# Block products 1 and 5 of the first MLP's first layer at two levels, with later index constants and whole kept weight tiles

## The chip, the cores and the metric

The kernel runs on one core of a Trainium2 chip. The metric is the device time of one execution in microseconds, lower is better. The core has five engines with queues of their own: TensorE (PE; its weight loads are PEld), VectorE (DVE), ScalarE (ACT), GpSimd (POOL) and SyncE (SP). SyncE, ScalarE and GpSimd also issue DMAs. All arithmetic here is in float32.

## The reference

Four sequences of 512 tokens with 512 features go through an attention block with two MLPs, and then through an adapter chosen per sequence.

```python
q, k, v = x @ Wq, x @ Wk, x @ Wv
attn = softmax(einsum('btd,bTd->btT', q, k) * 512 ** -0.5)
attn_out = einsum('btT,bTd->btd', attn, v) @ Wp + bp
cms_out = gelu(attn_out @ cW1 + cb1) @ cW2 + cb2 + one_hot(target_codes)[:, None, :]
modifier = gelu(concatenate([attn_out, cms_out], -1) @ mW1 + mb1) @ mW2 + mb2
x = clip(x + cms_out + modifier, 0.0, 1.0)

# adapter of sequence b, with its expert e = stream[b]
h = gelu(x @ W_down[e] + b_down[e]) @ W_up[e] + b_up[e] + x
out = (h - mean(h)) * rsqrt(var(h) + 1e-5) * ln_w[e] + ln_b[e]
```

The shapes: Wq, Wk, Wv, Wp 512x512; cW1 512x2048; cW2 2048x512; mW1 1024x2048; mW2 2048x512; W_down 3x512x256; W_up 3x256x512. The gelu is the exact one.

## The kernel before

**Pairs and block products.** The four sequences are worked on in two pairs. The two sequences of a pair stand side by side as the two column halves of one right-hand matrix, with features on the partitions. So each large product is a 2x2 block product, and it is computed in seven block products in place of eight. They are numbered 1 to 7: 1, 2, 3 and 4 take a block of the weights as it is or a sum of all four, 5, 6 and 7 take sums or differences. The right side has four differences t1 to t4 (`token_sums`, L185): t1 = b12 - b11, t2 = b22 - t1, t3 = b22 - b12, t4 = b21 - t2. The weights have four sums s1 to s4 (`weight_sums`, L178). Product 5 is s1 with t1, 6 is s2 with t2, 7 is s3 with t3, 3 is s4 with b22, 4 is a22 with t4, and 1 and 2 are a11 with b11 and a12 with b21. Products 1, 2 and 4 are called PLAIN because their weights are blocks of the original.

**Two levels.** In cW2, mW1 and mW2 each of these seven products is again split into seven (`inner`, L556). An inner product is 128 columns of weights against 256 columns of tokens. `inner` copies its first product from PSUM with ScalarE into `first`, and seven additions by VectorE (L573, or L575 with a bias) put the rest together. Their order is fixed: 1, 5, 6, 7, 2, 3, 4. The layer of cW1 (`c1_layer`, L638) has one level only: per product two groups g of four tiles, each tile two matmuls of width 512 (L663). There products 1 and 5 are copied out by ScalarE (L669, L671), and the others are added by VectorE (`combine_first_tile`, L677).

**Weight sums ahead of time.** GpSimd computes all sums of cW1, cW2, mW1 and mW2 while attention runs, and stores them in DRAM (`c1_kept`, `c2_kept`, `m1_kept`, `m2_kept`). `expansion` (L311) holds cW1 (`expand_c1`, L200), cW2 and mW1. `late_expansion` (L320) holds mW2 and runs beside the first pair's mW1 layer. In `expand` (L267) a product that is not PLAIN is stored by three DMAs: two for its own columns, one for its sums. `inner_weights` (L326) loads a tile by SyncE into one of four `wslot` buffers of 1792 floats per partition, seven blocks each; a group of mW1 uses two such tiles.

**The front.** Wq and Wk are transposed and multiplied into one matrix, `w_qk`. Then x is transposed (`transposed`, L356; `evacuate` L102 copies from PSUM, in turn by VectorE and ScalarE), and `pair_product` (L453, matmuls at L469) multiplies w_qk by the pair. Its outer loop is over the two row halves r of each block, its inner one over the products 1, 2, 5, 6, 7, 3, 4. Then come scores and softmax (L496 to L519), and a second pair product. Small constants stand ahead of the first transposes of x in the program: positions, expert indices and one-hot targets (L406 to L430, L437 to L440), each a few elements wide and done by VectorE. Sequences 2 and 3 of x are loaded at the start by ScalarE's and SyncE's queues (L140).

**Order.** The program is recorded through a tile framework that sets semaphores and orders each engine's queue. `tc.keep_in_program_order` pins an instruction where it stands. Buffers rotate: eight PSUM banks (`bank`) and four `wslot`.

**The MLPs.** Per pair: cW1 layer, cW2 layer (`second_layer`, L786, matmuls L812), mW1 layer (`m1_layer`, L713, matmuls L728), mW2 layer (`second_layer` again). Between the last two, x^T is loaded from DRAM and added to `cms` by GpSimd (L1012 to L1017); `m_last` (L861) reads the sum from product 5 of the mW2 layer on, which is the third of its seven. The adapters of the first pair run in steps between the groups of the second pair's cW1 layer. The last pair's adapters stand at the end (`adapter`, L904): transposes, down, up, and per tile of 128 tokens the normalisation, with multiplication by ln_w on VectorE (L961), addition of ln_b on GpSimd (L962), and the store by SyncE (L963). The fourth tile has a shorter form on VectorE alone (L949, L953).

Of the kernel before, what the change touches and what calls it, by code (L numbers as in the profile page):

```python
# [18 lines left out]
def kernel(  # L19
# [51 lines left out]

    FIRST = (1, 5, 6, 7, 2, 3, 4)
# [23 lines left out]
    wslot = [const.tile([P, 1792], F32, name=f"wslot{i}") for i in range(4)]  # L96
# [43 lines left out]
    for b in range(2, B):  # L140
        x_rows.append(load_x(b, (nc.scalar, nc.sync)[b % 2], x_places[b]))

# [53 lines left out]


    c1_kept = [spill.tile([P, 4, 2, 256], F32, name=f"c1_kept{j}") for j in range(4)]

    def expand_c1(j):  # L200
        raw = slot[4 + j % 2].rearrange("p (c h n) -> p c h n", c=4, h=2)
        for h in range(2):
            nc.gpsimd.dma_start(
                out=raw[:, :, h, :],
                in_=cW1[:, h * HH + j * 256 : h * HH + (j + 1) * 256].rearrange(
                    "(c p) n -> p c n", p=P
                ),
            )
        s = (part.rearrange("p c n -> p (c n)"), slot[1])[j % 2].rearrange(
            "p (k c n) -> p k c n", k=4, c=2  # L210
        )
        weight_sums(
            raw[:, 0:2, 0, :], raw[:, 2:4, 0, :], raw[:, 0:2, 1, :], raw[:, 2:4, 1, :],
            s[:, 0], s[:, 1], s[:, 2], s[:, 3],
        )
        nc.gpsimd.dma_start(out=c1_kept[j], in_=s)
# [4 lines left out]
    KEPT = {1: 0, 2: 1, 4: 2, 5: 3, 6: 4, 7: 5, 3: 6}  # L221
    PLAIN = {1: (0, 0), 2: (1, 0), 4: (1, 1)}

    def kept(name, units):
        return {
            (p, u): spill.tile([P, 4 if p in PLAIN else 7, 2, P], F32, name=f"{name}_{p}_{u}")
            for p in range(1, 8)
            for u in range(units)
        }
# [4 lines left out]
    turn = [0]  # L234

    def four(t):
        return t.rearrange("p (k c n) -> p k c n", k=4, c=2)
# [4 lines left out]
    def block_sums(t):  # L242

        return t.rearrange("p (c n) -> p c n", c=4)

    def split(t):
        return [t[:, :1024], t[:, 1024:2048]]

    flat_mod, flat_part = ([t.rearrange("p c n -> p (c n)") for t in ts] for ts in (mod, [part]))
    spare = [split(flat_part[0]), [first.rearrange("p c n -> p (c n)")]]  # L250
    spare = [sums_of(t) for ts in spare for t in ts]

# [14 lines left out]
    def expand(unit, raw, outer, places, then):  # L267

        src, is_first, dst, u = unit
        raw = [t.rearrange("p (c n) -> p c n", c=4) for t in raw]  # L270
        s1, s2, s3, s4 = (block_sums(t) for t in outer)
        a11, a12, a21, a22 = (
            raw[0][:, :, :256], raw[1][:, :, :256], raw[0][:, :, 256:], raw[1][:, :, 256:]
        )
        nc.gpsimd.tensor_tensor(s1, a21, a22, ALU.add)
        nc.gpsimd.tensor_tensor(s2, s1, a11, ALU.subtract)
        nc.gpsimd.tensor_tensor(s3, a11, a21, ALU.subtract)
        nc.gpsimd.tensor_tensor(s4, a12, s2, ALU.subtract)
        blocks = {1: a11, 2: a12, 4: a22, 5: s1, 6: s2, 7: s3, 3: s4}
        for i, (p, a) in enumerate(blocks.items()):  # L280
            if i == len(PLAIN):

                then()
            to = places[i % len(places)]
            weight_sums(
                a[:, 0:2, :P], a[:, 2:4, :P], a[:, 0:2, P:], a[:, 2:4, P:],
                to[:, 0], to[:, 1], to[:, 2], to[:, 3],
            )
            d = dst[p, u]
            if p in PLAIN:  # L290
                nc.gpsimd.dma_start(out=d, in_=to)
            else:
                nc.gpsimd.dma_start(out=d[:, 0:2].rearrange("p k c n -> p (k c) n"), in_=a[:, :, :P])
                nc.gpsimd.dma_start(out=d[:, 2], in_=a[:, 2:4, P:])
                nc.gpsimd.dma_start(out=d[:, 3:7], in_=to)
            yield

    def expand_all(units, raw, outer, places):
        load_raw(*units[0][:2], units[0][3], raw)
        for n, unit in enumerate(units):  # L300

            def then():
                if n + 1 < len(units):
                    load_raw(*units[n + 1][:2], units[n + 1][3], raw)

            yield from expand(unit, raw, outer, places, then)
# [4 lines left out]
    def expansion():  # L311

        for j in range(4):
            expand_c1(j)
            yield
        c2_units = [(cW2, False, c2_kept, u) for u in range(2)]
        outer = split(slot[1]) + split(slot[3])
        yield from expand_all(c2_units + m1_units, slot[4:6], outer, spare)

    def late_expansion():  # L320

        outer = split(flat_mod[0]) + split(flat_mod[1])
        places = [sums_of(t) for t in split(slot[0])]
        yield from expand_all(m2_units, slot[6:8], outer, places)

    def inner_weights(src, is_first, store, p, u):  # L326

        w = next_weights().rearrange("p (k c n) -> p k c n", k=7, c=2)
        if p not in PLAIN:
            nc.sync.dma_start(out=w, in_=store[p, u])  # L330
            return w
        h, o = PLAIN[p]
        plain = w[:, 0:2].rearrange("p k c n -> p (k c) n")
        if is_first:
            at = o * HH + u * 256
            rows = src[h * V : (h + 1) * V, :].rearrange("(c p) n -> p c n", p=P)
            nc.sync.dma_start(out=plain, in_=rows[:, :, at : at + P])
            nc.sync.dma_start(out=w[:, 2], in_=rows[:, 2:4, at + P : at + 2 * P])
        else:
            at = o * 256  # L340
            rows = src[h * HH : (h + 1) * HH, :].rearrange("(c p) n -> p c n", p=P)
            for i in range(2):
                k = 4 * i + 2 * u
                nc.sync.dma_start(out=w[:, i], in_=rows[:, k : k + 2, at : at + P])
            nc.sync.dma_start(out=w[:, 2], in_=rows[:, k : k + 2, at + P : at + 2 * P])
        nc.sync.dma_start(out=w[:, 3:7], in_=store[p, u])
        return w
# [57 lines left out]

    pos = const.tile([P, NV], F32, name="pos")  # L406
    tc.keep_in_program_order(nc.vector.tensor_copy(pos, pos_i))

    code = const.tile([P, B], F32, name="code")
    tc.keep_in_program_order(nc.vector.tensor_copy(code, code_i))  # L410

    ex = const.tile([P, B], F32, name="ex")
    tc.keep_in_program_order(nc.vector.tensor_copy(ex, str_i))
    wrap = const.tile([P, B], F32, name="wrap")
    nc.vector.tensor_scalar(wrap, ex, 0.0, float(E), ALU.is_lt, ALU.mult)
    nc.vector.tensor_add(ex, ex, wrap)
    nc.vector.tensor_scalar(ex, ex, 0.0, float(E - 1), ALU.max, ALU.min)
    ex_v = const.tile([P, B], F32, name="ex_v")  # L420
    nc.vector.tensor_scalar(ex_v, ex, float(V), None, ALU.mult)
    ex_bn = const.tile([P, B], F32, name="ex_bn")
    nc.vector.tensor_scalar(ex_bn, ex, float(BN), None, ALU.mult)
    idx_e = const.tile([P, B], I32, name="idx_e")
    nc.vector.tensor_copy(idx_e, ex)
    idx_d = const.tile([P, B, NV], I32, name="idx_d")
    idx_u = const.tile([P, B, NB], I32, name="idx_u")
    for b in range(B):
        nc.vector.tensor_scalar(idx_d[:, b, :], pos, ex_v[:, b : b + 1], None, ALU.add)
        nc.vector.tensor_scalar(idx_u[:, b, :], pos[:, :NB], ex_bn[:, b : b + 1], None, ALU.add)  # L430

# [4 lines left out]

    target = const.tile([P, B, NV], F32, name="target")  # L437
    for b in range(B):
        nc.vector.tensor_scalar(target[:, b, :], pos, code[:, b : b + 1], None, ALU.is_equal)
        nc.vector.tensor_add(target[:, b, :], target[:, b, :], cb2_c)  # L440
# [12 lines left out]
    def pair_product(lhs, rhs, out, bias_c=None):  # L453

        for r in range(2):
            c11, c12, c21, c22 = (out[k][:, o + r, :] for o in (0, 2) for k in range(2))

            def total(dst, one, two, o):
                if bias_c is None:
                    add(dst, one, two)  # L460
                else:
                    nc.vector.scalar_tensor_tensor(
                        dst, one, bias_c[:, o + r : o + r + 1], two, ALU.add, ALU.add
                    )

            for p in (1, 2, 5, 6, 7, 3, 4):
# [11 lines left out]
                elif p == 2:  # L478
                    ps2 = ps
                elif p == 5:  # L480
                    nc.scalar.copy(c22, ps)
                elif p == 6:
                    add(c21, ps, c11)
                    total(c11, ps2, c11, 0)
# [38 lines left out]
    for pair in range(B // 2):  # L523
# [4 lines left out]
        for k in range(2):  # L528
            if s0 + k:
                transposed(chunks(x_rows[s0 + k]), xT[k])  # L530
            nc.scalar.dma_start(out=xT_kept[s0 + k], in_=xT[k])
        pair_product(lhs_qk, block_operands(*xT, mod), u)
        if pair == 0:
# [3 lines left out]
            lhs_vp = block_weights(w_vp, slot[2], nc.vector)  # L537
        steps(expanding, 6)
# [575 lines left out]
```

## Time and profile before

| what | us |
|---|---|
| median of 3 runs | 1232.78 (1230.43 to 1233.13) |
| profiled execution, its own time | 1232.73 |
| its span, first to last instruction | 1230.6 |

| stretch, us from the start | length | PE busy | DVE busy | POOL busy |
|---|---|---|---|---|
| 0 to 64.3: weights Q/K, x of pair 0, first pair product | 64.3 | 52.0 | 37.5 | 38.2 |
| 64.3 to 164.5: rest of attention, pair 0 | 100.2 | 98.7 | 48.7 | 95.1 |
| 164.5 to 284.5: attention, pair 1 | 120.0 | 114.3 | 69.0 | 119.6 |
| 284.5 to 380.6: cW1 layer, pair 0 | 96.1 | 96.1 | 60.8 | 53.7 |
| 380.6 to 465.2: cW2 layer | 84.6 | 84.6 | 79.4 | 3.4 |
| 465.2 to 634.4: mW1 layer | 169.2 | 169.2 | 129.9 | 96.8 |
| 634.4 to 720.7: mW2 layer | 86.3 | 85.4 | 84.0 | 23.2 |
| 720.7 to 848.1: cW1 layer of pair 1, with pair 0's adapters | 127.4 | 127.4 | 70.8 | 27.2 |
| 848.1 to 1102.1: cW2 and mW1 layers, pair 1 | 254.0 | 254.0 | 197.6 | 11.9 |
| 1102.1 to 1212.5: mW2 layer and start of the last adapters | 110.4 | 109.5 | 95.2 | 42.7 |
| 1212.5 to 1230.6: end of the last adapter | 18.1 | 7.1 | 10.8 | 7.8 |

The rows come from one query of busy time by stretches; the first and the last but one rows and pair 1's middle are sums of two. A busy TensorE is not TensorE at its peak: ends of matmuls are modelled, and its clock can be lowered. What costs time is a stretch in which TensorE's busy time is shorter than the stretch, and a stretch at a low clock.

### The profile page before, as it was taken

The page shows a single profiled execution, that of the slowest core. Times are in us where ns is not written, and L with a number is a line of the kernel's source. Part 1 is how long each engine was busy: PE and PEld are TensorE (multiplying, and loading weights), DVE is VectorE, ACT ScalarE, POOL GpSimd, SP SyncE. Part 2 cuts the span into 40 slices and gives each one's busy share as a digit, 9 for nine tenths or more (in the row PEclk, how much of TensorE's full clock was granted, in tenths as well). Part 3 has the DMA queues.
Part 4 walks back from the last instruction along what each step waited for, and adds up shares of the span by engine and source line. Part 5 has one row for each costly group of instructions (what it writes and reads, how often), then busy time and mean ns, then how long its engine had stood idle before and what let it go on. Part 6 is the DMA issues. An engine that isn't in the chain of part 4 may idle for free.

```text
span 1230.6 us, 12329 instructions
## 1 busy us (share of the span) xinstructions
PE 1198.2 (97%) x4497; PEld 838.7 (68%) x4497; DVE 883.7 (72%) x1101; ACT 211.9 (17%) x361; POOL 519.5 (42%) x542
## 2 busy tenths in 40 slices
PE   7899999999999999999999999999999999999996
PEld 5344444444447888888888864446888888888872
DVE  4763474464759896699699943769986578699957
ACT  1112111112141000002220023352000002220014
POOL 6689999999900006686310263100000000117124
PEclk9899999999999999999999999999999999999998
DMA  9943466549634657867645462223653444465601
GB/s 327 341 185 138 158 235 222 184 158 324 222 106 142 235 158 237 307 235 250 236 154 223 162 188 77 69 99 102 251 162 130 155 187 161 149 214 180 220 1 69
DMA packets 93212, 226.30 MB, mean 184 GB/s; under 512 B 8884, under 2 KB 45792, under 8 KB 90080
## 3 DMA queue, kind: packets, MB, share of 16 engines
q1 hardware_dynamic: 67264, 132.14, 31.7%
q0 software_dynamic: 22560, 80.79, 18.6%
q10 hardware_dynamic: 3328, 12.58, 2.6%
q8 instruction: 36, 0.59, 0.2%
q14 instruction: 24, 0.20, 0.0%
HBM read 166.75 MB, written 58.72 MB: 183 GB/s over the span
## 4 chain that ended last, share of the span: by engine, by line
PE 88%; DVE 10%; issue 1%; ACT 0%; DMA 0%; POOLq 0%; POOL 0%; DVEq 0%; ACTq 0%
PE i L728 28%; PE i L812 22%; PE c L663 16%; PE pair L469 7%; PE prod_ps L372 7%; PE scores L501 3%; DVE slot L192 2%; PE down_ps L920 2%; PE up_ps L932 2%; DVE hidden L748 2%; PE tr_ps L361 1%; DVE mod L192 1%; DVE mod L517 1%; DVE mod L573 1%; PE res_ps L911 1%
## 5 line engine op out<-in xcount | busy, mean ns | idle before, releaser
L728 PE MATMUL i<-slot,wslot 128*128 128x256 f32 x1184 | 260.8, 379 | 0.0
L728 PEld LDWEIGHTS i<-slot,wslot 128*128 128x128 f32 x1184 | 225.0, 190 | 30.6
L812 PE MATMUL i<-slot,wslot 128*128 128x256 f32 x896 | 204.1, 380 | 1.9 <-DVE mod L573 1.6
L812 PEld LDWEIGHTS i<-slot,wslot 128*128 128x128 f32 x896 | 169.7, 190 | 27.1 <-DVE mod L573 3.2
L812 PE MATMUL i<-hidden,wslot 128*128 128x256 f32 x576 | 132.1, 379 | 0.0
L663 PE MATMUL c<-slot,wslot 128*128 128x512 f32 x288 | 125.1, 592 | 0.0
L580 ACT COPY first<-i 128x256 f32<-128x256 f32 (+1 forms) x56 | 26.8, 479 | 551.0 <-PE i L812 284.0
L812 PEld LDWEIGHTS i<-hidden,wslot 128*128 128x128 f32 x576 | 109.4, 190 | 16.2 <-issue 1.4
L573 DVE TENSOR_TENSOR part<-i,part 128x512 f32<-128x512 f32 (+1 forms) x156 | 91.0, 591 | 39.5 <-PE i L728 27.2
L602 ACT ACTIVATE hidden<-hidden,bias 128x512 f32<-128x512 f32 x128 | 85.8, 715 | 100.7 <-DVE hidden L443 100.7
L1013 POOL DMA_DIRECT2D slot<-xT_kept x4 | 2.2, 558 | 236.5 <-PE i L728 214.4
L663 PEld LDWEIGHTS c<-slot,wslot 128*128 128x128 f32 x288 | 54.6, 190 | 68.4 <-issue 65.8
L443 DVE TENSOR_TENSOR hidden<-c,hidden 128x512 f32<-128x512 f32 x80 | 54.0, 685 | 55.4 <-PE c L663 55.3
L663 PE MATMUL c<-wide,wslot 128*128 128x512 f32 x160 | 69.3, 592 | 0.0
L265 POOL DMA_DIRECT2D slot<-in_L_cond_mW x24 | 18.1, 762 | 120.6 <-DVE slot L192 118.6
L1015 POOL TENSOR_TENSOR cms<-cms,slot 128x1024 f32<-128x1024 f32 x8 | 23.5, 2948 | 96.4 <-PE i L728 81.0
L192 DVE TENSOR_TENSOR slot<-hidden,slot 128x1024 f32<-128x1024 f32 x48 | 62.7, 1306 | 0.3
L192 DVE TENSOR_TENSOR slot<-hidden 128x1024 f32<-128x1024 f32 x48 | 62.7, 1306 | 0.0
L663 PEld LDWEIGHTS c<-wide,wslot 128*128 128x128 f32 x160 | 30.4, 190 | 37.8 <-issue 36.8
L501 PE MATMUL scores<-hidden,hidden 128*128 128x512 f32 x128 | 55.3, 592 | 0.0
L573 DVE TENSOR_TENSOR part<-i,first 128x512 f32<-128x512 f32 (+1 forms) x62 | 36.3, 589 | 26.1 <-PE i L728 16.6
L443 DVE TENSOR_TENSOR hidden<-hidden,hidden 128x512 f32<-128x512 f32 (+1 forms) x40 | 49.8, 1248 | 1.8
(241 smaller groups left out, 1799.3 us busy)
## 6 DMA issues: line engine op xcount, KB each, us to landing
wslot<-m_kept SPq DMA_DIRECT2D x48, 896.0 KB
wslot<-m_kept SPq DMA_DIRECT2D x36, 512.0 KB
wslot<-c_kept SPq DMA_DIRECT2D x16, 896.0 KB
slot<-in_L_cond_mW POOLq DMA_DIRECT2D x24, 512.0 KB
m_kept<-part POOLq DMA_DIRECT2D x20, 512.0 KB
slot<-in_L_cond_cW POOLq DMA_DIRECT2D x16, 512.0 KB
wslot<-c_kept SPq DMA_DIRECT2D x32, 256.0 KB
wslot<-in_L_cond_mW SPq DMA_DIRECT2D x60, 128.0 KB
```

The lines of the kernel that those rows point to most:

```text
L192: i = eng.tensor_tensor(out_, one, two, ALU.subtract)
L372: nc.tensor.matmul(ps, lhsT=lhs(c)[:, d * P : (d + 1) * P], rhs=rhs(c), start=(c == 0), stop=(c == 3),)
L443: nc.vector.tensor_tensor(dst, a, b, ALU.add)
L469: nc.tensor.matmul(ps, lhsT=lhs[p][:, c, r * P : (r + 1) * P], rhs=rhs[p][:, c, :], start=(c == 0), stop=(c == 1),)
L501: nc.tensor.matmul(ps, lhsT=u[:, c, t * P : (t + 1) * P], rhs=xT[:, c, :], start=(c == 0), stop=(c == NV - 1),)
L573: nc.vector.tensor_tensor(dst, ps, other, ALU.add)
L580: nc.scalar.copy(c1, p1)
L602: nc.scalar.activation(block[:, t, :], block[:, t, :], AF.Gelu, bias=bias_c[:, 8 * half + t : 8 * half + t + 1],)
L663: nc.tensor.matmul(ps, lhsT=lhs(c, t), rhs=rhs[p][:, c, :], start=(c == 0), stop=(c == 1),)
L728: nc.tensor.matmul(out_ps[:, j, :], lhsT=a[j][:, KEPT[q], c, :], rhs=now[q][:, c, :], start=(c == 0), stop=(c == 1),)
L748: i = nc.vector.tensor_tensor(out_[:, tiles, :], one[:, tiles, :], two[:, tiles, :], ALU.subtract)
L812: nc.tensor.matmul(ps[:, :256], lhsT=a[k // 2][:, KEPT[q], k % 2, :], rhs=now[q][:, k, :], start=(k == 0), stop=(k == 3),)
```

## The change

It does seven things.

1. In the cW1 layer products 1 and 5 are split a second time: each of two groups takes seven inner products of 128 columns of weights and 256 tokens on a contraction of 128, two tiles each. `inner` puts them together, with `mod[0]` for the copy. Product 2 comes first now and is copied out by ScalarE; product 1 is put together in `h[2]` and added to `h[0]`. Two more sets of four small differences (`inner_sums`) are made by VectorE. `wslot` grows to 2048 floats, and `expand_c1` makes the inner sums for products 1 and 5.
2. `pair_product` runs over the products outside and over the row halves inside. Both transposes of a pair are made before the stores of x^T.
3. The small constants are made after the first pair product, in `constants()`.
4. Sequences 2 and 3 of x are loaded by GpSimd, behind the first loads of cW1.
5. A kept tile holds the whole block of 1024 floats and its sums of 1024, so that one DMA stores it and one loads it; `expand` makes the products in another order.
6. x^T is added to `cms` by an accumulating DMA instead of a load and two additions.
7. In the last adapter GpSimd takes both the multiplication and the addition of tiles 0 and 1, and VectorE both of tile 2.

```diff
+    FIRST_C = (2, 1, 5, 6, 7, 3, 4)
-    wslot = [const.tile([P, 1792], F32, name=f"wslot{i}") for i in range(4)]
+    wslot = [const.tile([P, 2048], F32, name=f"wslot{i}") for i in range(4)]
-    for b in range(2, B):
-        x_rows.append(load_x(b, (nc.scalar, nc.sync)[b % 2], x_places[b]))
...
+    def expand_c1(u, then):
...
+        weight_sums(
+            raw[0][:, 0, 0, :], raw[0][:, 1, 0, :], raw[1][:, 0, 0, :], raw[1][:, 1, 0, :], *inner_sums
+        )
+        nc.gpsimd.dma_start(out=c1_inner[1, u], in_=slot[1][:, 1024:])
...
+        weight_sums(s1[:, 0, 0, :], s1[:, 0, 1, :], s1[:, 1, 0, :], s1[:, 1, 1, :], *inner_sums)
+        nc.gpsimd.dma_start(out=c1_inner[5, u], in_=slot[1])
...
-            (p, u): spill.tile([P, 4 if p in PLAIN else 7, 2, P], F32, name=f"{name}_{p}_{u}")
+            (p, u): spill.tile([P, 1024 if p in PLAIN else 2048], F32, name=f"{name}_{p}_{u}")
...
-            if p in PLAIN:
-                nc.gpsimd.dma_start(out=d, in_=to)
-            else:
-                nc.gpsimd.dma_start(out=d[:, 0:2].rearrange("p k c n -> p (k c) n"), in_=a[:, :, :P])
-                nc.gpsimd.dma_start(out=d[:, 2], in_=a[:, 2:4, P:])
-                nc.gpsimd.dma_start(out=d[:, 3:7], in_=to)
...
+        def plain(*blocks):
+            for p, a, t in blocks:
+                inner_sums(a, t[:, 1024:])
+                keep(p, t[:, 1024:])
+                yield
...
+        def full(*sums):
+            for p, t in sums:
+                inner_sums(block(t[:, :1024]), t[:, 1024:])
+                keep(p, t)
+                yield
...
+        load_c1(0)
+
+        for b in range(2, B):
+            x_rows.append(load_x(b, nc.gpsimd, x_places[b]))
...
+    def constants():
+
+        tc.keep_in_program_order(nc.vector.tensor_copy(pos, pos_i))
...
     def pair_product(lhs, rhs, out, bias_c=None):
-        for r in range(2):
-            c11, c12, c21, c22 = (out[k][:, o + r, :] for o in (0, 2) for k in range(2))
...
-            for p in (1, 2, 5, 6, 7, 3, 4):
+        for p in (1, 2, 5, 6, 7, 3, 4):
+            for r in range(2):
+                c11, c12, c21, c22 = (out[k][:, o + r, :] for o in (0, 2) for k in range(2))
...
             lhs_vp = block_weights(w_vp, slot[2], nc.vector)
+            constants()
...
+        one = {1: inner_sums(0, b11)}
+        minus(t1, b12, b11)
+
+        def rest():
+            one[5] = inner_sums(1, t1)
+            minus(t2, b22, t1)
+            yield
+            minus(t3, b22, b12)
+            minus(t4, b21, t2)
+            yield
...
-        for p in FIRST:
+        two_level, one_level, rest = rhs
+        for p in FIRST_C:
             for g in range(2):
                 w = next_weights()
-                if p in (1, 2, 4):
-                    k, o = {1: (0, 0), 2: (1, 0), 4: (1, 1)}[p]
+                if p in (1, 5):
...
+                    def matmuls(q, ps):
+                        out_ps = ps.rearrange("p (j n) -> p j n", j=2)
+                        for j in range(2):
+                            nc.tensor.matmul(
+                                out_ps[:, j, :],
+                                lhsT=a[:, place[q], j * P : (j + 1) * P],
+                                rhs=two_level[p][q][:, 0, :],
+                                start=True,
+                                stop=True,
+                            )
+                        return out_ps
...
+                    inner(
+                        matmuls,
+                        [[v[:, o, pair_of, t, :] for t in range(2)] for o in range(2)],
+                        256, tmp=mod[0],
+                    )
+                    if p == 1:
+                        for tiles in (pair_of, slice(4 + 2 * g, 6 + 2 * g)):
+                            add(h[0][:, tiles, :], h[0][:, tiles, :], h[2][:, tiles, :])
+                            gelu(h[0], 0, cb1_c, range(tiles.start, tiles.stop))
+                    yield
+                    continue
...
-            nc.vector.tensor_mul(h, h, aff[:, 1, :])
-            nc.gpsimd.tensor_tensor(h, h, aff[:, 2, :], ALU.add)
+
+            scale = nc.gpsimd if final and t < 2 else nc.vector
+            shift_by = nc.vector if final and t == 2 else nc.gpsimd
+            scale.tensor_tensor(h, h, aff[:, 1, :], ALU.mult)
+            shift_by.tensor_tensor(h, h, aff[:, 2, :], ALU.add)
...
         for s in range(2):
-            nc.gpsimd.dma_start(out=in_rows[2 + s], in_=xT_kept[2 * pair + s])
-            for d in (slice(0, 2), slice(2, 4)):
-                nc.gpsimd.tensor_tensor(
-                    cms[s][:, d, :], cms[s][:, d, :], in_rows[2 + s][:, d, :], ALU.add
-                )
+            nc.gpsimd.dma_start(out=cms[s], in_=xT_kept[2 * pair + s], accum_op=ALU.add)
```

## The prediction

> **What bounds the kernel now.** I read the page first, then TensorE's waits, then the chain of waits in order of time, then busy time by short stretches and the timeline where the waits lie.
>
> ```profile
> PE 1198.2 (97%) x4497; PEld 838.7 (68%) x4497; DVE 883.7 (72%) x1101; ACT 211.9 (17%) x361; POOL 519.5 (42%) x542
> ...
> PEclk9899999999999999999999999999999999999998
> ...
> PE 88%; DVE 10%; issue 1%; ACT 0%; DMA 0%; POOLq 0%; POOL 0%; DVEq 0%; ACTq 0%
> ```
>
> TensorE is the bound: 97% busy, 88% of the chain. So time goes only where matmuls go, where a gap of TensorE closes, or where its clock rises. Who makes it wait:
>
> ```profile
> PE pair L469 <- DVE hidden L106: 5.1, 1, 5.1
> PE pair L469 <- DVE mod L192: 5.1, 3, 2.3
> ...
> PE i L812 <- DVE mod L573: 1.6, 4, 0.4
> ```
>
> Columns: total us, times, longest. 10.2 us lie in the Q/K pair products (L469). From 280 us to 1213 us all waits add up to 1.8 us, none of them on a DMA. Around the first Q/K product, by stretches (length; PE, PEld, DVE, ACT, POOL busy; clock, DMA share, GB/s):
>
> ```profile
> 29.30:34.30 5.00, 0.00 (x0) 0.00 (x0) 4.95 (x19) 0.00 (x0) 2.44 (x3) 0.98 1.03 406
> 34.30:36.00 1.70, 1.69 (x2) 0.84 (x3) 1.67 (x4) 0.67 (x2) 1.14 (x1) 0.50 1.07 394
> ...
> 41.30:43.60 2.30, 0.00 (x0) 0.00 (x0) 2.27 (x3) 0.59 (x1) 2.28 (x3) 1.00 1.03 427
> 43.60:46.00 2.40, 2.40 (x4) 1.16 (x5) 2.15 (x1) 0.00 (x0) 2.34 (x3) 0.65 0.98 406
> ```
>
> Each gap is paid twice: TensorE stands, then runs at 0.50 to 0.65 of its clock. In the first gap VectorE works through the small constants, some of them very slowly, and x's evacuation waits behind them:
>
> ```profile
> 26.35 4.13 DVE L418 TENSOR_TENSOR ex<-ex,wrap 128x4 f32<-128x4 f32 x1
> ...
> 34.31 5.26 PE L469 MATMUL pair<-hidden,cms 128*128 128x512 f32 x8 [5.09 <-DVE hidden L106]
> ```
>
> Rates come from the chain, where these stages run without a gap (each written matmul makes two records):
>
> ```profile
> 140.59 24.03 PE pair L469 x56
> ...
> 284.62 96.13 PE c L663 x224
> ...
> 465.36 169.21 PE i L728 x784
> ```
>
> So a record of width 512 costs 96.13/224 = 0.429 us, one of width 256 costs 169.21/784 = 0.216 us, and an undisturbed pair product 24.03 us. The end is a chain over VectorE, GpSimd and SyncE:
>
> ```profile
> 1224.96 0.68 DVE L961 TENSOR_TENSOR hidden<-hidden,wide 128x512 f32<-128x512 f32 x1
> 1225.73 1.26 POOL L962 TENSOR_TENSOR hidden<-hidden,wide 128x512 f32<-128x512 f32 x1 [2.09 <-DVE hidden L961]
> 1227.02 0.33 SPq L963 DMA_DIRECT2D out<-hidden  x1
> ```
>
> **What the Trainium skill says.** "TensorE: Matmul & The Clock Gate", section "What's actually happening": the array's clock is halved after about 3.4 us of idleness and comes back after about as much work. The trace agrees in kind (0.50 after a 5.0 us gap), but already a 2.3 us gap brings 0.65; the measurement decides. "SBUF — State Buffer", section "Who interferes with whom": a VectorE instruction with two SBUF inputs, or in a two-port mode, contends with GpSimd for a port pair, and the loser blocks for the whole instruction; one PSUM and one SBUF input do not contend. The trace agrees: the four-element add above took 4.13 us while GpSimd added back to back. "DMA: Bandwidth & Descriptors", section "SWDGE vs HWDGE vs iDMA": a DMA that accumulates can only be issued by GpSimd. No run here shows one yet.
>
> **The change part by part.** The sum is made against the profiled execution's own 1232.73 us (span 1230.6), which is within 0.1 us of the median of 1232.78.
>
> *Two levels for products 1 and 5.* One product of cW1 takes 2 groups x 4 tiles x 2 = 16 matmuls of width 512, 32 records: 13.73 us. At two levels it is 2 x 7 x 2 = 28 of width 256, 56 records: 12.09 us; the built order of instructions shows these 28. 1.65 us less, for two products and two pairs: **-6.6 us**. For it VectorE gets seven additions per group (about 0.62 us in a row, as L443's 0.68 and L573's 0.59 show) where ScalarE copied, and for product 1 two additions of 128x1024 (1.25): 6.9 us per group of product 1, 4.3 of product 5, against 6.04 on TensorE. TensorE can run ahead by eight PSUM banks; walking the built order with these durations, a bank comes free 1 us or more before it is wanted in pair 0 (half of that if GpSimd stretches the additions), and in pair 1, where the adapters' steps lie between, the tightest are within 0.5 us. I charge **+0.5**. The operands cost eight more subtractions of 128x256 (some 0.4 each), under the 13.7 us of product 2, which now comes first and needs none.
>
> *Constants later, and both row halves of one product in a row.* Before, from the end of the transposes at 29.2 to the end of the product at 64.3: 35.1 us, where 24.03 suffice; 11.1 are lost. After, no constant stands before the evacuation, and the first difference is wanted after two products of two halves, 6.86 us, not 3.43. What is late next: two block sums stand before x's copies and GpSimd is busy at that time; at 1.6 us each (L182 took 1.8) TensorE starts about 1.5 us late, and the second difference may be 1 us late: -11.1 + 2.5 = **-8.6**. Pair 1: 167.96 to 196.91 is 28.95 against 24.03; less 0.5 for a late difference, **-4.4**. The constants move beside the first scores: some 11 us of VectorE as stretched before, 4 if not, at tile 0 of eight. VectorE's step per tile was 2.35 us (86.92 to 89.27) against 3.43 of TensorE, so it catches up some 1 us per tile. Between 0 and 7 us, taken **+1.5**. The like wait in pair 1 (VectorE's 5.03 us at 212.84, then a 2.5 us gap and 1.6 us of low clock) depends on where GpSimd's 2.36 us additions fall: between -4 and +4, taken **0**.
>
> *Whole kept tiles, x's later rows by GpSimd.* GpSimd issues seven DMAs fewer per expanded unit, and its work ends earlier; it is hidden (first kept tile of cW2 wanted at 380). The weights of an unfolded product are 1 MB, not 896 KB; two per 12.09 us. Hidden as SyncE's queue always waited for TensorE and not the reverse: **0**, to +30 if a load is late. x2 and x3 are wanted at 164; moved past the first loads of cW1 they land far earlier: 0.
>
> *Accumulating DMA for x.* It replaces a 1 MB load and GpSimd's two additions (2.95 us each), which stand on VectorE's port in the second MLP's second layer: there TensorE lost 1.8 us in five waits, and a little rate. It has from the last reader (about 600) to 670 in pair 0, and some 35 us in pair 1; the plain load took 8 us (633.15 to 641.15). Its speed is not shown: at double that it is still hidden; late by 30 us it would cost as much. **-1.8** (0 to -2.9).
>
> *Tail.* Tiles 0 and 1 lose a VectorE multiplication each (1.2 us), tile 2 ends with VectorE's 0.68 in place of GpSimd's 1.26 plus a handover, while GpSimd takes four operations, ending by about 1224. **-1.2** (0 to -2).
>
> Sum: -6.6 + 0.5 - 8.6 - 4.4 + 1.5 - 1.8 - 1.2 = -20.6, so 1232.7 - 20.6 = **1212**.
>
> **Rivals.**
> 1. VectorE becomes the bound where it is loaded. Constants beside the scores stop it for their 11 us (7 after catching up, 1.6 of clock), and the first layer's groups of product 1 run at VectorE's pace with stretched additions. For it: 72% busy, ops at three times their length. Against: both places have slack of tiles or banks. -20.6 + 9 gives 1221.
> 2. The front gains nothing, as GpSimd's sums of cW1 now stretch VectorE where it was free: only -6.6, -1.8, -1.2 and little else: 1224. For it: GpSimd works through from 18.8. Against: the removed work exceeds what stretching can add.
> 3. Slower: loads of the weights. Place: the 56 steps of cW2, mW1, mW2 (28 per pair) which take two 1 MB tiles per 12.09 us from four buffers, 173 GB/s where 152 were wanted. It decides from 20.6/56 = 0.37 us per step; at 0.6 it gives 1232.7 - 20.6 + 34 = 1246. For it: DMAs are 0.73 busy in the first half of mW1's layer in pair 0 (465 to 547 us). Against: no wait on a DMA after 5 us, and longer rows per packet.
> 4. The change not doing what it says: excluded for the matmuls by the built order.
>
> **How the numbers follow.** Forecast 0.66 (own range 1205 to 1218); rivals 1 and 2 together 0.20; rival 3 with a late accumulate 0.09; a chance near nothing lost or won, 0.05. The range of 8 in 10 leaves out rival 3 and takes most of 1 and 2: 1203 to 1222. 0.2% is 2.5 us, about what a measurement can tell here. Faster 0.88, the same 0.03, slower 0.09.
>
> **What would show it.** Right: the first layer's stretch without adapters about 93 us where 96.1 were; two Q/K products of 24 to 27 us with a clock near 1; no wait on a DMA in the MLPs; no GpSimd additions to cms; the last out DMA some 1 us sooner after the last matmul. Wrong: TensorE waiting on VectorE in the new inner products, on a weight tile, or before the transposes of the softmax.

## The result: slower, 1246.85 us, with the profile after

The changed kernel takes 1246.85 us (median of 6 runs, 1236.63 to 1254.08) against 1232.7 (1229.03 to 1236.08): ratio 1.0101, 95% interval 1.0069 to 1.0133. A second measurement gave 1241.38 and 1.0105 (1.0045 to 1.0165). The forecast was 1212. Times here are medians of all runs, while the ratios leave out runs more than 1.5% above a kernel's fastest (none of these twelve), so a ratio is not the quotient of two medians. The spread is news too: 18 us between runs, where the kernel before has 7. The profiled execution is the shortest, 1236.63 us with a span of 1234.8, so it shows only 3.9 of the 14 us lost.

From the page of the changed kernel (busy time of the engines, TensorE's clock, the chain that ended last):

```profile
PE 1193.0 (97%) x4593; PEld 858.1 (69%) x4593; DVE 932.8 (76%) x1164; ACT 209.3 (17%) x355; POOL 474.2 (38%) x501
...
PEclk9998979999999999999999999999999999999998
...
PE 80%; DVE 12%; issue 3%; DMA 3%; ACT 1%; POOL 1%; ACTq 0%; DVEq 0%; POOLq 0%
```

TensorE's work fell by 5.2 us (1198.2 to 1193.0) and the span still grew; its share of the chain went from 88 to 80%. So it waits more. TensorE's waits (total us, times, longest):

```profile
PE prod_ps L425 <- DVE hidden L107: 13.9, 6, 9.3
...
PE tr_ps L414 <- DVE hidden L499: 3.8, 2, 2.3
PE tr_ps L414 <- DVE hidden L520: 3.6, 4, 3.1
PE i L852 <- DMA wslot<-in_L_cond_mW: 1.5, 1, 1.5
PE i L746 <- DVE hidden L632: 0.9, 3, 0.4
```

The 10.2 us before the Q/K products have shrunk to 1.4. In their place stand 9.3 us after the first softmax and 7.4 at the end of the first pair's V product, both on VectorE. By stages, from the start of TensorE's groups in the timelines (us; the last two columns are the two kernels with GpSimd's sums cut, experiment 3):

| stage | before | after | before, no sums | after, no sums |
|---|---|---|---|---|
| start to first scores | 80.5 | 70.8 | 69.8 | 69.6 |
| first scores to first V product | 59.9 | 71.4 | 60.0 | 59.9 |
| V product to pair 1's scores | 56.5 | 64.3 | 51.6 | 51.6 |
| those scores to the first c layer | 87.5 | 86.2 | 84.0 | 84.0 |
| first c layer | 96.1 | 95.1 | 96.1 | 92.8 |
| to pair 1's c layer | 340.2 | 340.5 | 340.1 | 338.7 |
| pair 1's MLPs and the end | 509.8 | 506.5 | 509.9 | 506.0 |

The c layer is that of cW1. The two gains forecast for the front arrived (9.7 us in pair 0; the second Q/K product takes 24.8 us instead of 28.95). Next to them 11.5 us are lost in the first softmax and 12.0 between the V product and the second Q/K product. Here is the first loss, as VectorE and GpSimd show it in the timeline (start, duration, instruction):

```profile
87.52 0.16 DVE L573 RECIPROCAL inv<-total 128x1 f32<-128x1 f32 x1 [0.84 <-ACT mod L571]
87.72 8.26 DVE L574 TENSOR_SCALAR mod<-mod,inv 128x512 f32<-128x512 f32 x1
95.90 0.67 DVE L566 TENSOR_REDUCE top<-scores 128x1 f32<-128x512 f32 x1
```

```profile
85.89 0.57 POOL L301 DMA_DIRECT2D c_kept<-part  x1 [0.30 <-POOL part L181]
86.48 2.35 POOL L298 TENSOR_TENSOR slot<-part,slot 128x1024 f32<-128x1024 f32 x1
88.80 2.34 POOL L298 TENSOR_TENSOR wide<-slot 128x1024 f32<-128x1024 f32 x1
91.10 0.71 POOL L178 TENSOR_TENSOR wide<-slot 128x256 f32<-128x256 f32 x1
...
94.51 0.71 POOL L179 TENSOR_TENSOR slot<-slot,slot 128x256 f32<-128x256 f32 x1
95.18 0.57 POOL L301 DMA_DIRECT2D c_kept<-wide  x1
95.77 0.78 POOL L180 TENSOR_TENSOR slot<-slot 128x256 f32<-128x256 f32 x1
```

The softmax's multiplication, which takes 0.49 us where nothing holds it, takes 8.26: from inside a run of eight additions of GpSimd's until GpSimd leaves the run to issue a DMA. It ends 0.2 us after that issue, so its last 0.49 us begin inside it. The reduction behind it, which reads PSUM, is untouched. The first loss is made of this meeting and four smaller ones (1.99 to 3.47 us) in the same softmax: TensorE waits 9.3 us and then runs 4.1 us at a clock of 0.50. The second loss, at the end of the V product, has the same shape:

```profile
155.83 7.45 DVE L499 TENSOR_TENSOR hidden<-hidden 128x512 f32<-128x512 f32 x1
163.20 0.68 DVE L499 TENSOR_TENSOR hidden<-pair,hidden 128x512 f32<-128x512 f32 x1
163.92 0.75 DVE L520 SCALAR_TENSOR_TENSOR hidden<-pair,bias,hidden 128x512 f32<-128x512 f32 x1
164.58 3.67 DVE L499 TENSOR_TENSOR hidden<-hidden 128x512 f32<-128x512 f32 x1
...
170.70 5.42 DVE L520 SCALAR_TENSOR_TENSOR hidden<-hidden,bias 128x512 f32<-128x512 f32 x1
```

An add whose inputs both lie in SBUF (hidden, hidden) takes 3.67 to 7.45 us; the same add with one input in PSUM (pair) takes 0.68 beside it.

The theory to be tested, called the port theory below: a VectorE instruction whose inputs all lie in SBUF can wait for a whole *run* of GpSimd's additions, most often until GpSimd issues a DMA, and the change, which took such issues away, left more of GpSimd's time in unbroken runs. Counted in GpSimd's timelines from the first scores to 285 us (additions less than 0.25 us apart are one run), the kernel before has 7 runs of 3 us or more, 70 us together in a stretch of 204.5, and the changed one 22, 128 us together in 214; GpSimd issues 92 DMAs there before and 62 after. The longest single run is the old kernel's (16.6 us against 11.5), so it is not the longest run that grew. Where they lie counts too: the first of the old seven begins at 119.0 us, behind the first softmax, while four of the new ones (from 78.8 to 107.1 us) lie in it. Of the 12 VectorE instructions above 2.7 us up to 330 us of the changed kernel's trace, 10 end within 1.1 us of the start of such a DMA issue, of which there is one in 3.5 us on average. Rivals: the constants beside the scores (rival 1 of the prediction), late weight tiles (rival 3), and the order of the row halves.

### The profile page after: what moved, and what is told of

It is laid out like the page before. It is cut to its first block, busy times and chain, and to the rows that moved or that the text cites. A ratio compares the mean times of both kernels' runs of the same rounds, so it can differ in the third digit from the quotient of the medians.

```text
span 1234.8 us, 12399 instructions
## 1 busy us (share of the span) xinstructions
PE 1193.0 (97%) x4593; PEld 858.1 (69%) x4593; DVE 932.8 (76%) x1164; ACT 209.3 (17%) x355; POOL 474.2 (38%) x501
## 4 chain that ended last, share of the span: by engine, by line
PE 80%; DVE 12%; issue 3%; DMA 3%; ACT 1%; POOL 1%; ACTq 0%; DVEq 0%; POOLq 0%
PE i L936 27%; PE i L852 25%; PE c L788 9%; PE prod_ps L425 7%; PE pair L526 5%; DVE mod L574 3%; DVE hidden L499 2%; PE down_ps L1044 2%; PE i L746 1%; PE up_ps L1056 1%; DVE mod L190 1%; DVE hidden L520 1%; DMA wslot<-in_L_cond_mW 1%; PE tr_ps L414 1%; DMA wslot<-m_kept 1%
## 5 line engine op out<-in xcount | busy, mean ns | idle before, releaser
L788 PE MATMUL c<-slot,wslot 128*128 128x512 f32 x224 | 96.9, 592 | 0.0
L788 PEld LDWEIGHTS c<-slot,wslot 128*128 128x128 f32 x224 | 42.6, 190 | 53.6 <-issue 51.7
L1007 POOL DMA_INDIRECT slot<-in_L_cond_b_up,idx_e x3 | 4.3, 1425 | 187.7 <-PE i L852 187.0
L1007 POOL DMA_INDIRECT slot<-in_L_cond_W_down,idx_d x12 | 15.5, 1292 | 149.7 <-PE i L936 88.5
L632 DVE TENSOR_TENSOR hidden<-i,hidden 128x512 f32<-128x512 f32 x80 | 53.7, 686 | 14.3 <-PE i L852 13.2
L190 DVE TENSOR_TENSOR slot<-hidden,slot 128x1024 f32<-128x1024 f32 x48 | 58.5, 1219 | 0.3
L190 DVE TENSOR_TENSOR slot<-hidden 128x1024 f32<-128x1024 f32 x48 | 58.5, 1218 | 0.0
L499 DVE TENSOR_TENSOR hidden<-c,hidden 128x512 f32<-128x512 f32 x64 | 43.3, 687 | 18.9 <-PE c L788 18.9
L499 DVE TENSOR_TENSOR hidden<-hidden,hidden 128x512 f32<-128x512 f32 (+2 forms) x48 | 55.5, 1161 | 1.2
L499 DVE TENSOR_TENSOR hidden<-part,hidden 128x2048 f32<-128x2048 f32 x20 | 47.4, 2371 | 0.5
```

The costliest lines, as they stand in the source:

```text
L190: i = eng.tensor_tensor(out_, one, two, ALU.subtract)
L499: nc.vector.tensor_tensor(dst, a, b, ALU.add)
L632: nc.vector.tensor_tensor(dst, ps, other, ALU.add)
L788: nc.tensor.matmul(ps, lhsT=lhs(c, t), rhs=one_level[p][:, c, :], start=(c == 0), stop=(c == 1),)
```

## The experiments

All are beside the kernel before on the same chip; the ratio is to the kernel before.

| run | us (lowest to highest) | ratio, 95% interval |
|---|---|---|
| after_again | 1241.38 (1240.6 to 1254.1) | 1.0105, 1.0045 to 1.0165 |
| act_mul | 1221.67 (1213.1 to 1240.8) | 0.9846, 0.9811 to 0.988 |
| split_stores | 1230.2 (1213.4 to 1236.3) | 0.9911, 0.9875 to 0.9947 |
| v_rows | 1240.81 (1230.2 to 1261.1) | 1.003, 1.0003 to 1.0058 |
| after_small | 1204.03 (1203.2 to 1204.4) | 0.9758, 0.9709 to 0.9808 |
| before_small | 1212.64 (1211.6 to 1213.4) | 0.9828, 0.9778 to 0.9879 |
| before_act | 1227.31 (1225.7 to 1234.7) | 0.9964, 0.9946 to 0.9981 |
| no_sbuf_only | 1212.35 (1209.7 to 1221.9) | 0.9854, 0.979 to 0.9918 |
| old_constants | 1242.67 (1237.0 to 1250.8) | 1.0079, 1.0053 to 1.0106 |
| split_old_constants | 1224.03 (1217.0 to 1231.7) | 0.9891, 0.9827 to 0.9954 |
| no_sbuf_only_split | 1209.66 (1206.2 to 1215.3) | 0.9784, 0.9744 to 0.9824 |
| iota_breaks | 1240.5 (1232.5 to 1250.6) | 1.0049, 1.0027 to 1.0072 |

**1. A second trace of the changed kernel.** No edit.

> The changed kernel unchanged, for a second trace. If the lost time is chance meetings of VectorE instructions that use SBUF alone with GpSimd's runs of additions, the stages before the first MLP (to the first c product) should differ from the first trace by several us, in other places, and the rest by under 1 us; time 1236 to 1254. If the loss is a fixed one (the constants, or the order of the halves), the same gaps of 9.3 us before the first prod_ps after the scores and 11 us before the second Q/K product come again within 1 us. If late weight tiles make the longer runs, a wait of TensorE on a wslot DMA grows from 1.5 us to over 5.

The two large gaps came again at the same places (11.2 us after the first softmax, up to 1.5 and 4.5 at the V product's end), so on this point the "fixed loss" reading looked as good as the port's. Elsewhere the trace differs: the first c layer took 96.4 us instead of 95.1. The wait on a weight tile shrank from 1.5 us to 0.3 while the span grew by 4 us: late weights are not it. Both traces are of runs near the short end, so where the runs of 1250 us and more lose their time is not shown.

**2. The softmax's multiplication on ScalarE.**

```diff
-            nc.vector.tensor_scalar(p, p, inv, None, ALU.mult)
+            nc.scalar.activation(p, p, AF.Copy, scale=inv)
```

> The softmax's multiplication by 1/sum goes from VectorE to ScalarE (16 instructions of 128x512). Port theory: the 8.26 us multiplication and its like are gone, the gap before the first prod_ps falls from 9.3 to under 1.5 us, with its 2.7 us of low clock, and the pair 1 gap of 2.8 too: 11 to 14 us faster than the changed kernel, unless the V product's end (12 us) grows. Constants theory: the gap stays above 5 us. Late-weights theory: no change.

About 20 us faster than the changed kernel by the second median, 31 by the ratios, where 11 to 14 were expected, and faster than the kernel before. The first softmax ends without a large gap, with the constants still beside it: as a fixed cost, the constants theory falls. But runs reach up to 1241. No trace shows one of those; the trace of a run of 1221.67 us shows a gap that moved: TensorE waits 5.7 us before the first Q/K product, on a block sum of W_qk that met a run of five additions of GpSimd's. That sum stands in the changed kernel as well; in its trace that sum came to stand behind x's first copies, and took 5.59 us of which TensorE lost 0.8.

The same edit in the kernel before:

> The kernel before with the softmax's multiplication on ScalarE alone. If the softmax of the kernel before meets GpSimd in pair 1 only (the 5.03 us multiplication), it gains that gap of 2.5 us and its low clock, 1.6: 1228 to 1231. If ScalarE's multiplication is a gain of its own, apart from the port, it gains as much as in the changed kernel: 1214 to 1222.

It gains 4 to 5 us, a quarter or less of what the edit gives in the changed kernel: what it removes is the meeting with GpSimd, of which the kernel before had one large one in its softmax.

**3. GpSimd's sums cut to 16 columns, in both kernels.** This leaves out most of each weight sum of the MLPs; stores and waits stay. The edit, without the like cut of each unit's four large sums:

```diff
+        if eng is None:
+            a11, a12, a21, a22, s1, s2, s3, s4 = (
+                t[..., :16] for t in (a11, a12, a21, a22, s1, s2, s3, s4)
+            )
         eng = eng or nc.gpsimd
```

> The changed kernel with GpSimd's weight sums cut to 16 columns of each block (the rest of the sums is left out, the stores, loads and waits stay), so that GpSimd hardly adds. Port theory: no SBUF-only instruction of VectorE above 2 us before the first MLP, the gaps before the first prod_ps after the scores and before the second Q/K product under 1 us each; from the profile's 1236.6, less 11.5, 11.5, 2.3 and some 2 in the first c layer and 2 in the front: about 1207 (1203 to 1211), all runs within 4 us. If the constants or the order of the halves by themselves cost the time: above 1225.

> The same cut of GpSimd's sums in the kernel before (the rest of the sums is left out). Port theory: its gaps of 5.1, 2.3, 2.75 and 2.5 us with their low clock go in good part: 1216 to 1224, so that the changed kernel without sums is some 10 to 15 us faster than it, as the prediction had it, and the two kernels' losses to the port differ by 14 or more. If the change is slower for another reason, the two kernels without sums keep the difference of 8 us in the old sense.

This decides between GpSimd's additions and the rest. Without most of them the changed kernel takes 1204.03 us and the kernel before 1212.64, with 2 us of spread or less: the change is worth 8.6 us, and GpSimd's additions cost the kernel before 20 us and the changed one 43 (1246.85 - 1204.03; 37 by its second measurement). VectorE's groups between 60 and 292 us say whom they cost. The changed kernel, groups of instructions (busy us, mean ns):

```profile
L574 DVE TENSOR_SCALAR mod<-mod,inv 128x512 f32<-128x512 f32 x16 | 34.7, 2171 | 0.5
...
L499 DVE TENSOR_TENSOR hidden<-hidden 128x512 f32<-128x512 f32 x8 | 20.5, 2561 | 0.1
...
L499 DVE TENSOR_TENSOR hidden<-pair,hidden 128x512 f32<-128x512 f32 x18 | 12.2, 684 | 19.0 <-PE pair L526 12.2 <-issue 6.7
```

The same groups with the sums cut:

```profile
L505 DVE TENSOR_TENSOR hidden<-pair,hidden 128x512 f32<-128x512 f32 x18 | 12.4, 687 | 25.6 <-PE pair L532 17.5 <-issue 8.0
...
L580 DVE TENSOR_SCALAR mod<-mod,inv 128x512 f32<-128x512 f32 x16 | 8.3, 517 | 0.5
...
L505 DVE TENSOR_TENSOR hidden<-hidden 128x512 f32<-128x512 f32 x8 | 5.5, 684 | 0.1
```

And of the kernel before, with its sums:

```profile
L517 DVE TENSOR_SCALAR mod<-mod,inv 128x512 f32<-128x512 f32 x16 | 16.3, 1020 | 0.5
...
L443 DVE TENSOR_TENSOR hidden<-pair,hidden 128x512 f32<-128x512 f32 x23 | 15.9, 690 | 30.6 <-PE pair L469 29.8
...
L443 DVE TENSOR_TENSOR hidden<-hidden 128x512 f32<-128x512 f32 x10 | 8.2, 817 | 0.1
```

Read the means downwards: 2171, 517, 1020 ns for the multiplication and 2561, 684, 817 for the SBUF-only add, while the add that reads PSUM is 684, 687, 690 in all three. The kernel before came out 3.4 us under the range expected, so that the two differ by 8.6 us and not by 10 to 15. The table of stages shows where: with the sums cut its front takes 69.8 us against 69.6, with the constants where they were and the old order of the halves. In the front neither of them cost more than 0.2 us by itself; both had only met GpSimd.

**4. Which part made the runs longer: stores after every two additions.**

```diff
...
+        nc.gpsimd.dma_start(out=place[:, :512], in_=to[:, :512])
+        nc.gpsimd.tensor_tensor(s3, a11, a21, ALU.subtract)
+        nc.gpsimd.tensor_tensor(s4, a12, s2, ALU.subtract)
+        nc.gpsimd.dma_start(out=place[:, 512:], in_=to[:, 512:])
```

> Each kept tile of cW2, mW1 and mW2 leaves GpSimd in two or three stores again, one after every two additions (18 stores in a unit where the changed kernel has 8 and the kernel before 15). If whole tiles are the cause, as they let GpSimd add for longer without a break, VectorE's longest blocked instruction falls from 8.3 us to about 4 or less, and the time by 8 to 20 us, to 1215 to 1230. If the cause is only where GpSimd's additions lie (the gathers of bd gone from the first scores), the blocked instructions stay as long, the time within 5 us of the changed kernel. Cost of the stores: GpSimd's expansion ends some 45 us later, about 300 us, hidden.

1230.2 us: 11 to 17 us come back by the medians, some 23 by the ratios, with 0.57 us more of GpSimd's time per store; the additions of its first expansion end at 347.6 us instead of 318.6, hidden. The multiplication's mean falls from 2171 to 1307 ns, the SBUF-only add's from 2561 to 997, runs of 3 us or more from 22 to 16 and from 128 us together to 70, the longest from 11.5 us to 7.4. The expectation of 4 us for the longest blocked instruction was too low: a softmax multiplication takes 6.42 us and one difference of 128x1024 (1.22 us with the sums cut) takes 8.02. So breaking the runs gives back most of the added loss, or all of it. It is not the old state again, as the kernel before had 15 stores per unit and this one has 18, and it doesn't help everywhere. In its trace the V product's stage falls from 64.3 to 51.6 us, but the front rises from 70.8 to 77.8 and the first softmax stays at 72.0 (71.4). There it is the small constants that met GpSimd, as rival 1 of the prediction had it; one of them, 0.22 us where nothing holds it, waited past one DMA issue and got in at the next:

```profile
88.87 6.10 DVE L495 TENSOR_SCALAR idx_d<-pos,ex_v 128x4 int32<-128x4 f32 x1
```

```profile
89.56 0.56 POOL L305 DMA_DIRECT2D c_kept<-part  x1
90.13 2.35 POOL L302 TENSOR_TENSOR slot<-part,slot 128x1024 f32<-128x1024 f32 x1
92.44 2.35 POOL L302 TENSOR_TENSOR wide<-slot 128x1024 f32<-128x1024 f32 x1
94.73 0.57 POOL L274 DMA_DIRECT2D c_kept<-part  x1
```

**5. The constants in their old place.** With them eight gathers of an expert's bias go back from about 320 us to the first third of the attention: 10 us in which GpSimd doesn't add.

```diff
+    constants()
+
+    transposed(chunks(x_rows[0]), big[2])
...
-            constants()
```

> The changed kernel with the constants back before the first x tile's transposes; the eight gathers of bd then stand in GpSimd's queue in the first third of the attention again, not at 320 us. If the gathers (10 us in which GpSimd doesn't add) were what kept the first softmax of the kernel before free, the gap of 9.3 us before the first prod_ps after the scores falls to under 3, and the front loses 4 to 9 us again before the first Q/K product: within 6 us of the changed kernel. If whole tiles alone matter, that gap stays, and the time is 4 to 9 us longer than the changed kernel's.

> The changed kernel with both: stores after every two additions and the constants in their old place. If these two carry the added loss, the loss to the port is that of the kernel before, 20 us, on the 1204 that the changed kernel takes without sums: 1221 to 1228. If the order of the row halves or the c layer's inner sums carry a good part, it stays above 1232.

Alone no gain: the wait after the first softmax falls from 9.3 us to 4.7, not under 3, and the front pays 9.3 us again. With the stores split as well 1224.03, inside the range expected; but 6 us below split_stores, over four runs that spread by 15, don't establish a gain of its own.

**6. The V product with the row halves outermost.** The old loop for that product alone.

> The product for V and output alone has the row halves outermost again, as before; Q/K keeps the new order. If the order of the halves bunches VectorE's work at the end of that product (four SBUF-only instructions in its last 10 us instead of two), the 11.97 us lost between it and the second Q/K product fall to under 5. If only the meeting with GpSimd's run matters, the loss depends on where the run falls and stays between 0 and 12 us, for a mean gain of half. The 9.3 us gap after the first scores stays in both.

1240.81, over runs that spread by 31 us: the halves' order cannot be told from chance here.

**7. Can any instruction break a run?** A small iota behind most additions of GpSimd's.

```diff
...
+            (eng or nc.gpsimd).tensor_tensor(out_, one, two, op)
+            if eng is None:
+                pause()
```

> The changed kernel with a small iota (128x1, GpSimd, some 0.15 us) behind most additions of a kept tile, and no other store. If any instruction between two additions opens the port, VectorE's blocked instructions end at the next iota, and none is above 4 us outside the runs of the three large additions (2.35 us each): 1222 to 1236. If it needs a pause as long as a DMA's issue (0.57 us), they stay at up to 8 us, and the time at 1238 to 1252.

As a rule it doesn't. A multiplication of VectorE's in that run, to 102.14 us, and GpSimd's timeline beside it:

```profile
93.55 8.59 DVE L581 TENSOR_SCALAR mod<-mod,inv 128x512 f32<-128x512 f32 x1
```

```profile
97.60 0.12 POOL L103 IOTA rest_i<- 128x1 int32 x1
97.69 0.71 POOL L185 TENSOR_TENSOR wide<-slot 128x256 f32<-128x256 f32 x1
...
100.58 0.12 POOL L103 IOTA rest_i<- 128x1 int32 x1
100.67 0.71 POOL L185 TENSOR_TENSOR slot<-slot,slot 128x256 f32<-128x256 f32 x1
101.33 0.57 POOL L308 DMA_DIRECT2D c_kept<-wide  x1
101.91 0.25 POOL L103 IOTA rest_i<- 128x1 int32 x1
```

Four iotas between the additions let nothing in; the 0.57 us of a DMA's issue did. The time, 1240.5 us, and the mean of the multiplication, 2570 ns, are no better than the changed kernel's. But two instructions of the same trace (4.08 us from 215.78, 3.79 from 299.74) ended just behind an iota, with no DMA issue near.

**8. A version that beats both.** Beside edit 2, product 5 of the attention's pair products stays in PSUM until both of its sums are made, and W_qk's sums are held behind the copies of x.

```diff
                 elif p == 5:
-                    nc.scalar.copy(c22, ps)
+                    ps5[r] = ps
...
-                    add(c12, c22, c21)
+                    add(c12, ps5[r], c21)
...
-                    total(c22, c22, c21, 2)
+                    total(c22, ps5[r], c21, 2)
```

> The changed kernel in which the instructions that TensorE waits for read PSUM or run on ScalarE: the softmax's multiplication on ScalarE, product 5 of the attention's pair products left in PSUM until its two sums are made, and W_qk's block sums put behind the copies of the first two x tiles. Port theory: the waits at the end of the V product (10 us with their clock) and of 5.7 us before the first Q/K product go as well: 1206 to 1216, with a spread smaller than the 18 us of the changed kernel. Constants theory or late weights: no better than with the multiplication alone, 1221.

> The kernel in which TensorE waits for no SBUF-only instruction in the softmax and the V product, and the stores after every two additions as well. What is left to gain over 1212 is the front and low clock, 3 to 5 us: 1206 to 1213. If the later end of the expansion (45 us) makes a kept tile of cW2 late, or the stores the loads, it is slower than 1214.

1212.35 and, with edit 4 too, 1209.66 us: 2.2% under the kernel before (interval 1.8 to 2.6%), and 5.6 us above the kernel without sums. All of TensorE's waits on VectorE that are above 0.5 us in the first of the two:

```profile
PE pair L532 <- DVE mod L190: 2.9, 1, 2.9
PE prod_ps L425 <- DVE hidden L107: 1.8, 4, 0.5
```

Of what costs TensorE more than 0.5 us, only the differences of x before product 5 are still caught there. In the trace of the second, its longest run (1215.27 us), TensorE waits 3.5 us behind the first softmax, where a constant took 6.10 us again, and 3.5 in all on the differences. The spread fell to 12 and 9 us, not to nothing.

## Why the prediction was wrong, by its steps

- **Whole kept tiles, "GpSimd issues seven DMAs fewer per expanded unit, and its work ends earlier; it is hidden ... 0"** is the step that failed. It priced the DMA issues as GpSimd's own time, and at nothing what fewer breaks between GpSimd's additions do to VectorE. The issues were the openings through which VectorE most often got to SBUF: with fewer of them the cost of GpSimd's additions grew from 20 us to 37 or 43 (experiment 3), and 11 to 23 us of it came back when runs were broken again (experiment 4). How much of the growth is owed to whole tiles and how much to where the runs now fall, with another order of products and the gathers moved, stays open.
- **What the sum had right.** The terms that don't rest on VectorE and GpSimd meeting in the attention, -6.6 + 0.5 - 1.8 - 1.2, make -9.1, and without the sums the two kernels differ by 8.6; singly these terms are off by up to 1.6 us, as shown below. The others, -8.6 - 4.4 + 1.5 = -11.5, came out as a loss of 17 to 23.
- **Constants beside the scores, "some 11 us of VectorE as stretched before ... +1.5"**, and **the softmax, "0"**. In the changed kernel's traces the constants weren't the trouble in the first softmax (11.5 us lost): its own multiplications were. With split stores the constants were (experiment 4). The sum took VectorE's step per tile, 2.35 us, from 86.92 to 89.27 us of the old trace, where a DMA issue of GpSimd's followed every three additions or fewer; right behind it (91.5 to 101.5 us) GpSimd gathered instead of adding. That the gathers go along with the constants was visible in the built order and was not priced; experiment 5 halves the gap by putting them back, and its share in the total stays open.
- **The end of the V product** had no term. It lost 12.0 us: four SBUF-only adds with a run of GpSimd's on top. Whether the new order of the halves, which brings them together at the end, has a share was not settled (experiment 6).
- **Q/K pair 0, -8.6, and pair 1, -4.4**: measured -9.7 and -4.1 in the profiled execution, near the forecast but for the wrong reason. The time before was lost to GpSimd and not to the constants or the halves as such (experiment 3), so it could come back: 5.7 us of it did, in the traces of experiments 2 and 4.
- **Two levels for products 1 and 5, -6.6 + 0.5**: the matmuls are right to the tenth: without the sums the first c layer takes 92.8 us instead of 96.1, -3.3 as worked out for one pair. In the changed kernel only 1.0 came in pair 0; 0.9 us of waits there are VectorE's, which was behind after one difference of 128x256 that took 5.38 us (296.52 to 301.90) in a run of GpSimd's, and the rest of the 2.3 us missing is not accounted for. In pair 1, 2.0 came, with the sums and without.
- **Accumulating DMA, -1.8**: the second MLP's second layer, with the last sums of x, went from 86.3 to 84.6 us in pair 0 and by as much in pair 1 (112.4 to 110.7 up to VectorE's first addition from up_ps): -3.4, more than the range of 0 to -2.9 allowed. No wait on it is in the trace.
- **Tail, -1.2**: from VectorE's first addition from the last up_ps group to the last output DMA 12.5 us became 11.9: -0.6.
- **Rival 3** named 1246, nearly the time measured, with the wrong mechanism: one wait of 1.5 us on a weight tile. **Rival 1**, VectorE as the bound, had the place and not the size: it charged 9 us, and took the instructions stretched to be the constants alone.

The prediction cited the Trainium skill, "SBUF — State Buffer", section "Who interferes with whom", that the loser blocks for the whole instruction of the other, and it had the trace's 4.13 us beside it. Four microseconds among additions of 1.3 us already said that the loser waits for more than one of them; and that instruction ended at 30.48 us, just after GpSimd began to issue a DMA at 30.40. The runs agree with the page on who contends (the add that reads PSUM never did: 684 to 690 ns) and differ on how long: up to 8.3 us, beside eight additions.

## What to carry to other kernels

Before DMA issues or other pauses are taken off GpSimd to make it quicker, look at what VectorE does in them: an instruction of VectorE's with all its inputs in SBUF can wait out a whole run of additions. GpSimd's busy share doesn't show this: from the first scores to 285 us it was 98% before and 94% after, while the loss about doubled. Count the runs, and see where they fall. On the path of TensorE, where it can be done, keep one input in PSUM or give the work to ScalarE; this was worth more than the whole of this change. And where two VectorE durations of the same shape differ by several times in one trace, cutting the other engine's work to a sliver in both kernels shows what a change is worth by itself.

## What was not expected of the hardware

- A blocked VectorE instruction of 0.5 us waited up to 8.3 us, beside eight additions in a row, and got in at a DMA issue of 0.57 us; pauses of 0.12 us (an iota) between the additions mostly didn't let it in. It is no strict rule: an instruction of 7.45 us ended at 163.28, where GpSimd shows no DMA issue but an addition of 1.18 us instead of 0.72, and with split stores one waited past a DMA issue of 0.56 us (experiment 4).
- The two engines can also take turns. Where VectorE had three differences of 128x1024 one behind the other (142.97 to 148.16 us of the changed kernel), each took 1.74 to 1.86 us instead of 1.23, and GpSimd's additions of 128x256 1.58 to 1.70 instead of 0.72. What decides between the two ways is not shown: in the kernel before two of four such differences in a row took 3.11 and 3.86 us (from 169.03 and 172.25).
- The spread between runs came with GpSimd's additions: 18 us for the changed kernel and 7 for the one before, 1.2 and 1.8 with the sums cut.
